# Layer 0's scan: four state groups of one channel half in a row, and B brought to SBUF by DMA instead of to PSUM by a matmul

## The chip, the cores and the metric

The kernel runs on one core of a Trainium2 chip. The metric is the device time of one launch in microseconds (us). The kernel runs four layers one after the other in a single launch; the change touches only layer 0.

## The reference

Layer 0 works on `x` of shape (4, 96, 64, 64): 4 images, 96 channels, a sequence of 4096 positions. Two Mamba blocks are applied to each image, then a 1x1 convolution, a batch norm and a residual. Only the Mamba block matters here (192 inner channels, 16 states):

```python
xs, z = jnp.split(h @ in_w, 2, axis=-1)          # h: normalised sequence
xc = silu(causal_conv(xs))                       # 4 taps
dbl = xc @ xproj_w
dt, Bm, Cm = dbl[..., :6], dbl[..., 6:22], dbl[..., 22:]
delta = softplus(dt @ dt_w + dt_b)
dA  = exp(delta[..., None] * A)                  # (b, l, 192, 16)
dBx = delta[..., None] * Bm[:, :, None, :] * xc[..., None]
hstates = scan over l of  s = dA * s + dBx
y = einsum('blds,bls->bld', hstates, Cm) + Dp * xc
return (y * silu(z)) @ out_w
```

Everything is float32. Layers 1 to 3 (another state space layer, an attention layer, a deformable convolution layer) follow and are the same in both kernels.

## The kernel before

**Units and visits.** The sequence is cut into chunks of T = 512 positions. A *unit* is one chunk of one block of one image: 4 x 2 x 8 = 64 units, in order. The 192 channels are two *halves* (`hf`) of 96; the 16 states are four *groups* (`nq`) of 4. One *visit* `v` handles one half and one group: 96 channels x 4 states = 384 rows, laid out as 3 tiles (`q`, NG = 3) of 128 partitions (32 channels x 4 states). So a unit has 8 visits, numbered `m`; the list `ORDER` says which (group, half) each is: (0,0), (0,1), (1,0), (1,1), (2,0), (3,0), (3,1), (2,1).

**What a visit does.** `xR` holds delta*xc and `dR` holds delta, each replicated four times over the partitions; both are tiles of 128 x 3 x 512 in SBUF, loaded from a DRAM buffer `spread` by six DMAs per half (`replicate`, L537). Then:

- `states_in` (L557): one TensorE matmul with a selection matrix puts the four B rows of the group on 128 partitions, `Bb`, a PSUM tile of a pool with one buffer (`pb`). Two visits in a row of the same group share it.
- `inputs` (L566, the instruction is L571): VectorE multiplies `xR` by `Bb`, broadcast over the 3 tiles: `bt`, 128 x 1536.
- `decay` (L575, L582): ScalarE computes exp(A * dR) for one tile into PSUM (`a_ps`, 3 buffers).
- `states` (L594, L598): VectorE runs the scan of one tile in place in `bt`.
- `outputs` (L602): ScalarE saves the carry (L606), GpSimd multiplies `bt` by `Cb` (L607). `Cb` is C on 128 partitions, loaded by DMA into SBUF.
- `collect` (L611): TensorE sums over the states into `yp` (L621, L624); two visits later.

`bt` has 4 buffers, so the multiplication of a visit needs the `collect` of four visits before.

**Preparation.** `prepare` (L416) computes everything a unit needs before its visits: norm, convolution (L450, 16 matmul records), the projection (L471), `dbl`, softplus, and the gate. It is a generator with some 35 steps. It puts six large products on GpSimd per unit, all 96 x 1024 tensor_tensor with both inputs in SBUF: L465, L504, L509, L517, L528, and, in `finish` (L637), L640. On VectorE it puts L440 and two L497.

**What sets the order.** The order of layer 0 is written out by hand (`manual_schedule`). The main loop (L676) walks over the visits, four slots `q` = 0..3 each: slots 0 to 2 issue a scan and the decay two ahead, slot 3 issues `collect(v - 2)`, `outputs(v)` and `inputs(v + 1)`. The steps of `prepare` are dealt out one per slot; a unit's preparation begins `AHEAD` = 14 slots before the unit ahead of it starts (`PERIOD` is 32 slots). Each engine executes its own instructions in this order; DMAs of this layer are all issued from SyncE's queue (SP), also in order.

In the slots below, (m, q) is slot q of visit m of a unit.

Of the kernel before, what the change touches and what calls it, by code (L numbers as in the profile page):

```python
# [10 lines left out]
F32 = mybir.dt.float32  # L11
# [46 lines left out]
def host_arrays(inp):  # L58
# [16 lines left out]
    for at, n, src in ((0, 6, 0), (32, 16, 6), (64, 16, 22)):  # L75
        xp[:, :, at : at + n] = inp["L0_conv_xproj_w"][:, :, src : src + n]
# [18 lines left out]
    seln = np.zeros((128, 4, 128), f)  # L95
    for n in range(4):
        seln[32 + 4 * n + p % 4, n, p] = 1
    a["c_seln"] = seln
# [241 lines left out]
def layer0(k, X):  # L340
# [6 lines left out]
    ORDER = ((0, 0), (0, 1), (1, 0), (1, 1), (2, 0), (3, 0), (3, 1), (2, 1))  # L347
    LAST = {hf: max(m for m, o in enumerate(ORDER) if o[1] == hf) for hf in range(2)}
    with ExitStack() as es:
# [11 lines left out]
        seln = k.load(wp, "c_seln", (128, NQ, 128))  # L361
# [24 lines left out]
        def pool(name, bufs, **kw):  # L386
            return scan.enter_context(tc.tile_pool(name=f"l0{name}", bufs=bufs, **kw))
# [4 lines left out]
        pm, pa = pool("pm", 2, space=PSUM), pool("pa", 3, space=PSUM)  # L392
        pb, py = pool("pb", 1, space=PSUM), pool("py", 2, space=PSUM)
# [22 lines left out]
        def prepare(b, i, ch, st, before):  # L416
# [28 lines left out]
            xc = st["xc"] = p3.tile([C, 2, T], F32, name="xc")  # L445
# [9 lines left out]
            yield  # L455
            for hf, p in enumerate(ps):
                nc.scalar.activation(xc[:, hf], p[:C], AF.Identity, bias=k.v(f"conv_b{i}{hf}"))
                yield
# [17 lines left out]
            out = dram.tile([16, T], F32, name="out_states")  # L476
            nc.sync.dma_start(out, dbl[64:80])
# [47 lines left out]
            replicate(st, 0)  # L525
# [4 lines left out]
            st["Cb"] = [cp.tile([128, T], F32, name="Cb") for _ in range(NQ)]  # L530
            for nq, t in enumerate(st["Cb"]):
                nc.sync.dma_start(
                    t, out[PS * nq : PS * nq + PS].unsqueeze(0).to_broadcast([32, PS, T])
                )
            yield

        def replicate(st, hf):  # L537

            for n, name in enumerate(("dR", "xR")):
                t = st[name, hf] = p3.tile([128, NG, T], F32, name=name)  # L540
                for q in range(NG):
                    r = 96 * hf + 32 * q
                    nc.sync.dma_start(
                        t[:, q], st["spread"][n, r : r + 32].unsqueeze(1).to_broadcast([32, PS, T])
                    )

        units = [(b, i, ch) for b in range(B) for i in range(2) for ch in range(NCH)]
        V = NT * len(units)
        sts = [{} for _ in units]
        carries, bts, Bbs, dec, skips = {}, {}, {}, {}, {}  # L550

        def at(v):

            u, m = divmod(v, NT)
            return (sts[u], units[u], *ORDER[m])

        def states_in(v):  # L557

            st, _, nq, _ = at(v)
            if v and v % NT and ORDER[v % NT - 1][0] == nq:  # L560
                Bbs[v] = Bbs[v - 1]
                return
            Bb = Bbs[v] = pb.tile([128, T], F32, name="Bb")
            nc.tensor.matmul(Bb, seln[:, nq], st["dbl"], start=True, stop=True)  # L564

        def inputs(v):  # L566

            st, _, nq, hf = at(v)
            bt = bts[v] = bp.tile([128, NG, T], F32, name="bt")
            Bb = Bbs[v]  # L570
            nc.vector.tensor_mul(  # L571
                bt, st["xR", hf], Bb.unsqueeze(1).to_broadcast([128, NG, T])
            )
# [28 lines left out]
        def outputs(v):  # L602

            st, _, nq, hf = at(v)
            bt = bts[v]
            nc.scalar.copy(carry_of(v), bt[:, :, T - 1])  # L606
            nc.gpsimd.tensor_mul(  # L607
                bt, bt, st["Cb"][nq].unsqueeze(1).to_broadcast([128, NG, T])
            )

        def collect(v):  # L611
# [11 lines left out]
            for q in range(NG):  # L623
                nc.tensor.matmul(  # L624
                    st["yp", hf][32 * q : 32 * q + 32],
                    red,
                    bt[:, q],
                    start=False,
                    stop=v % NT == LAST[hf],
                )  # L630

        def output(u, hf):

            st, (b, i, ch) = sts[u], units[u]
            nc.scalar.copy(st["xc"][:, hf], st["yp", hf])
# [24 lines left out]
        PERIOD, AHEAD = 4 * NT, 14  # L660

        with tc.manual_schedule():
# [4 lines left out]
            replicate(sts[0], 1)  # L667
            states_in(0)
# [7 lines left out]
            for v in range(V + 7):  # L676
                u, m = divmod(v, NT)
                for q in range(4):
# [4 lines left out]
                    if (m, q) in ((4, 1), (5, 0), (5, 1), (5, 3)):  # L683
                        next(task, None)
# [4 lines left out]
                    if q == 1 and v + 1 < V:  # L689
                        states_in(v + 1)  # L690
                    if q == 1 and m in (1, 2) and 0 < u <= len(units):
                        output(u - 1, m - 1)
# [10 lines left out]
                    if q == 3:  # L703
                        outputs(v)
                        if m == LAST[0] and u + 1 < len(units):
                            replicate(sts[u + 1], 1)
                        if v + 1 < V:
                            inputs(v + 1)
# [1489 lines left out]
```

## Time and profile before

| | |
|---|---|
| time, median of 3 runs | 7859.52 us (7859.1 to 7862.05) |
| profiled execution, its own time | 7854.38 us |
| its span in the trace | 7852.6 us |
| granted TensorE clock, mean | 0.815 |
| layer 0 in the span | until about 3460 us |
| visits (L571) | 512, in 64 units |

Busy time in the stretch 500 to 3300 us of the span, all of it layer 0 in its steady course (2800 us):

| engine | busy us | share |
|---|---|---|
| TensorE (matmul) | 2147.5 | 77% |
| VectorE (DVE) | 2406.6 | 86% |
| ScalarE (ACT) | 1909.9 | 68% |
| GpSimd (POOL) | 2218.7 | 79% |
| DMA engines, mean share | | 29%, 97 GB/s |

How to read it: several engines are busy most of the time and hand tiles round in a ring, so no share by itself says what a change is worth; what counts is how long a unit takes and which wait ends last in it. The product L640 comes once per unit, so its start times mark the units: from 181.27 us (the first) to 3369.7 us (the 62nd) there are 61 units, (3369.7 - 181.27) / 61 = 52.27 us each. The last two units, which have less preparation beside them, are shorter (47.5 and 35.9 us).

### The profile page before, as it was taken

What the parts mean: (1) busy time and instruction counts of PE and PEld (TensorE: products, weight loads), DVE (VectorE), ACT (ScalarE), POOL (GpSimd) and SP (SyncE); (2) the same over time, 40 slices, a digit from 0 to 9 for tenths busy, and PEclk for the clock granted to TensorE, in tenths of its full rate; (3) what the DMA queues carried; (4) which work ended last, traced back from release to release, by engine and by line L of the source; (5) the groups of instructions that cost most, each with busy time, mean ns of one, the idle gap of its engine ahead of it and who ended that gap; (6) DMA issues with size and microseconds to landing.
All of it is one profiled execution on the core that took longest, in us unless ns stands there. A gap on an engine that the chain in (4) does not pass through costs nothing.

```text
span 7852.6 us, 76871 instructions
## 1 busy us (share of the span) xinstructions
PE 5919.8 (75%) x24218; PEld 2757.7 (35%) x24218; DVE 5718.9 (73%) x8127; ACT 3944.6 (50%) x7624; POOL 4694.6 (60%) x2915
## 2 busy tenths in 40 slices
PE   5777777777777777756666989898987577777774
PEld 1222222222222222224223646455554534443432
DVE  4888888888888888865886545455454477777787
ACT  4666666666666666643332556455555212121212
POOL 3787778777887788742444434334250067777775
PEclk8888888888888888878886888888888678787886
DMA  3233223223332223234222001010100155656555
GB/s 99 101 102 103 79 101 103 98 84 101 102 103 79 101 103 103 84 115 125 80 80 67 19 11 32 1 41 2 36 8 24 40 168 158 189 152 189 158 157 172
DMA packets 424414, 720.32 MB, mean 92 GB/s; under 512 B 188150, under 2 KB 190254, under 8 KB 419763
## 3 DMA queue, kind: packets, MB, share of 16 engines
q1 hardware_dynamic: 348710, 480.74, 19.7%
q0 software_dynamic: 73968, 227.47, 10.2%
q10 hardware_dynamic: 1328, 7.20, 0.2%
q8 instruction: 193, 3.16, 0.2%
q14 instruction: 215, 1.75, 0.1%
HBM read 567.04 MB, written 97.82 MB: 85 GB/s over the span
## 4 chain that ended last, share of the span: by engine, by line
PE 30%; DVE 19%; POOL 7%; ACT 6%; issue 6%; DMA 4%; SPq 1%; DVEq 0%; POOLq 0%; ACTq 0%
POOL sm L1993 5%; PE sc_ps L1069 3%; DVE bt L598 3%; PE mm_ps L450 2%; PE pT_ps L1118 2%; DMA sm<-table,ix 2%; DVE bt L571 2%; PE o_ps L1138 2%; DVE prod L2010 2%; DVE sm L2011 1%; PE Bb L564 1%; PE mm_ps L507 1%; PE m_ps L1527 1%; PE bc_ps L319 1%; DVE lp L886 1%
## 5 line engine op out<-in xcount | busy, mean ns | idle before, releaser
L607 POOL TENSOR_TENSOR bt<-bt,Cb 128x1536 f32<-128x1536 f32 x512 | 1761.9, 3441 | 674.3 <-issue 444.9
L598 DVE TENSOR_TENSOR_SCAN bt<-a_ps,carry,bt 128x512 f32<-128x512 f32 x1536 | 1865.2, 1266 | 58.5 <-ACT a_ps L582 11.4
L1993 POOL DMA_INDIRECT sm<-table,ix x1152 | 1098.4, 953 | 742.9 <-ACT maps L1669 346.3
L582 ACT ACTIVATE a_ps<-dR,w_l_A_log 128x512 f32<-128x512 f32 x1536 | 1053.6, 687 | 345.9 <-DVE bt L598 341.6
L571 DVE TENSOR_TENSOR bt<-xR,Bb 128x1536 f32<-128x1536 f32 x512 | 889.2, 1737 | 389.6 <-issue 186.9
L564 PE MATMUL Bb<-dbl,w_c_seln 128*128 128x512 f32 x640 | 446.5, 786 | 383.4 <-DVE bt L571 383.4
L1106 POOL TENSOR_TENSOR p<-p,rs 128x392 f32<-128x392 f32 x384 | 311.6, 839 | 476.8 <-DVE rs L1104 406.1
L450 PE MATMUL mm_ps<-h,Wk 96*128 96x512 f32 x1024 | 564.5, 714 | 11.0 <-issue 6.6
L624 PE MATMUL yp<-bt,w_c_red 128*32 128x512 f32 x3072 | 559.5, 634 | 6.0 <-POOL bt L607 6.0
L471 PE MATMUL mm_ps<-xc,w_l_xp 96*128 96x512 f32 x256 | 232.8, 1064 | 290.6 <-POOL xc L465 290.6
L2031 PE MATMUL sT_ps<-ident,sd 128*128 128x128 f32 (+1 forms) x896 | 212.9, 355 | 295.8 <-DVE sd L2014 175.7
L319 PE MATMUL bc_ps<-xs,w_l_bc 96*128 96x512 f32 x384 | 241.8, 763 | 215.1 <-DVE q L913 215.1
L1093 ACT ACTIVATE p<-p,rs 128x196 f32<-128x196 f32 x768 | 342.7, 449 | 83.6 <-DVE rs L1083 83.3
L450 PEld LDWEIGHTS mm_ps<-h,Wk 96*128 96x128 f32 x1024 | 240.0, 236 | 363.2 <-issue 333.1
L564 PEld LDWEIGHTS Bb<-dbl,w_c_seln 128*128 128x128 f32 x640 | 137.2, 242 | 655.7 <-DVE bt L571 496.6
L1916 PE MATMUL yb_ps<-X,w_l_base_w 96*128 96x504 f32 (+3 forms) x576 | 311.4, 706 | 0.3 <-ACT go L1930 0.3
L2010 DVE TENSOR_TENSOR prod<-sm,cws 128x960 f32<-128x960 f32 (+1 forms) x256 | 270.8, 1058 | 55.2 <-DMA sm<-table,ix 49.5
L2032 ACT COPY sT<-sT_ps 128x512 f32<-128x512 f32 (+1 forms) x256 | 121.8, 476 | 368.1 <-PE sT_ps L2031 368.1
L1126 DVE COPY pT<-pT_ps 98x512 f32<-98x512 f32 x256 | 176.0, 687 | 155.1 <-PE pT_ps L1118 147.7
L507 PE MATMUL mm_ps<-h,w_l_z_w 96*128 96x512 f32 x256 | 226.3, 1035 | 76.3 <-ACT w L503 76.3
L890 POOL TENSOR_SCALAR q<-lp 128x1024 f32<-128x1024 f32 x48 | 133.6, 2784 | 236.4 <-DVE lp L886 236.4
L1083 DVE CUSTOM_DVE_ANT_0 p<-sc_ps,bias 128x196 f32<-128x196 f32 x768 | 233.6, 353 | 49.6 <-PE sc_ps L1069 49.3
(372 smaller groups left out, 12615.3 us busy)
## 6 DMA issues: line engine op xcount, KB each, us to landing
dR<-spread SPq DMA_DIRECT2D x384, 256.0 KB
xR<-spread SPq DMA_DIRECT2D x384, 256.0 KB
Cb<-out_states SPq DMA_DIRECT2D x256, 256.0 KB
spread<-w SPq DMA_DIRECT2D x128, 192.0 KB
spread<-dx SPq DMA_DIRECT2D x128, 192.0 KB
table<-xT SPq DMA_DIRECT2D x256, 96.0 KB
own<-vd SPq DMA_DIRECT2D x512, 36.8 KB
toep<-l_toep SPq DMA_DIRECT2D x12, 1536.0 KB
```

The costliest lines, as they stand in the source:

```text
L319: self.nc.tensor.matmul(ps[:, s], lhsT, rhs[:, s], start=k == 0, stop=k == len(terms) - 1)
L450: nc.tensor.matmul(p, Wk[:, i, t, hf], h[:, t : t + T], start=t == 0, stop=t == 3)
L564: nc.tensor.matmul(Bb, seln[:, nq], st["dbl"], start=True, stop=True)
L571: nc.vector.tensor_mul(bt, st["xR", hf], Bb.unsqueeze(1).to_broadcast([128, NG, T]))
L582: nc.scalar.activation(dec[n], st["dR", hf][:, q], AF.Exp, scale=A[:, i, nq, hf, q : q + 1])
L598: nc.vector.tensor_tensor_scan(t, dec.pop(n), t, carry_of(v)[:, q : q + 1], ALU.mult, ALU.add)
L607: nc.gpsimd.tensor_mul(bt, bt, st["Cb"][nq].unsqueeze(1).to_broadcast([128, NG, T]))
L624: nc.tensor.matmul(st["yp", hf][32 * q : 32 * q + 32], red, bt[:, q], start=False, stop=v % NT == LAST[hf],)
L1093: nc.scalar.activation(ps[n][:, h, i], ps[n][:, h, i], AF.Exp, scale=-1.0, bias=rs[n][:, 0, h, i : i + 1], accum_out=rs[n][:, 1, h, i : i ...
L1106: nc.gpsimd.tensor_tensor(ps[n][:, h], ps[n][:, h], rs[n][:, 1, h].unsqueeze(2).to_broadcast([128, 2, KW * KW]), ALU.mult,)
L1993: nc.gpsimd.indirect_dma_start(sm[u][:, t].rearrange("p q c -> p (q c)"), None, samples[m // NN % 2], bass.IndirectOffsetOnAxis(ap=ix[m][: ...
L2010: nc.vector.tensor_mul(p, v[:, :, 2:4], w_[:, :, 2:4])
```

## The change

- The visits of a unit go through the four groups of half 0 and then the four groups of half 1 (`m % NQ`, `m // NQ`); `ORDER` and `LAST` are gone.
- `states_in`, its selection matrix and its PSUM pool are gone. B rows are written to DRAM together with the C rows (one DMA of 32 rows where 16 were written before), and `broadcast` loads the 128-partition copies of both by DMA into SBUF, four `Bb` and four `Cb` per unit, 6 buffers each. `inputs` multiplies `xR` by this `Bb`.
- `dR` and `xR` have 2 buffers each instead of 3: one per half. The loads of the next unit's half 0 are issued at slot (3, 1) and those of half 1 at (7, 1).
- The matmul results of the preparation get a third PSUM buffer (`pm`).
- `AHEAD` is 24 instead of 14, so every step of the preparation comes 10 slots earlier; the steps of `finish` and `output` move to other slots.

The core of the diff (line numbers of the kernel before are those above; in the changed kernel the products and scans are L554 for L571, L581 for L598, L590 for L607, and the preparation's products L458, L497, L502, L510, L520 and L623 for L465, L504, L509, L517, L528 and L640):

```diff
-    ORDER = ((0, 0), (0, 1), (1, 0), (1, 1), (2, 0), (3, 0), (3, 1), (2, 1))
...
-        pm, pa = pool("pm", 2, space=PSUM), pool("pa", 3, space=PSUM)
-        pb, py = pool("pb", 1, space=PSUM), pool("py", 2, space=PSUM)
+        pm, pa = pool("pm", 3, space=PSUM), pool("pa", 3, space=PSUM)
+        py = pool("py", 2, space=PSUM)
...
-            out = dram.tile([16, T], F32, name="out_states")
-            nc.sync.dma_start(out, dbl[64:80])
+            rows = st["rows"] = dram.tile([2, 16, T], F32, name="rows")
+            nc.sync.dma_start(rows.rearrange("c n t -> (c n) t"), dbl[48:80])
...
-                t = st[name, hf] = p3.tile([128, NG, T], F32, name=name)
+                t = st[name, hf] = p2.tile([128, NG, T], F32, name=name)
...
+        def broadcast(st, c, nq):
+
+            name = ("Bb", "Cb")[c]
+            t = st[name, nq] = cp.tile([128, T], F32, name=name)
+            src = st["rows"][c, PS * nq : PS * nq + PS]
+            nc.sync.dma_start(t, src.unsqueeze(0).to_broadcast([32, PS, T]))
...
-            return (sts[u], units[u], *ORDER[m])
-
-        def states_in(v):
...
-            Bb = Bbs[v] = pb.tile([128, T], F32, name="Bb")
-            nc.tensor.matmul(Bb, seln[:, nq], st["dbl"], start=True, stop=True)
+            return (sts[u], units[u], m % NQ, m // NQ)
...
             bt = bts[v] = bp.tile([128, NG, T], F32, name="bt")
-            Bb = Bbs[v]
+            Bb = st["Bb", nq]
...
-        PERIOD, AHEAD = 4 * NT, 14
+        PERIOD, AHEAD = 4 * NT, 24
...
-                    if q == 1 and v + 1 < V:
-                        states_in(v + 1)
-                    if q == 1 and m in (1, 2) and 0 < u <= len(units):
-                        output(u - 1, m - 1)
+                    if q == 1 and m == 6 and u < len(units):
+                        output(u, 0)
+                    if q == 1 and m == 2 and 0 < u <= len(units):
+                        output(u - 1, 1)
+                    if u + 1 < len(units):
+                        if q == 1 and m in (3, 7):
+                            replicate(sts[u + 1], m // NQ)
+                        if q == 3 and m in (4, 5):
+                            for nq in (2 * m - 8, 2 * m - 7):
+                                broadcast(sts[u + 1], 0, nq)
+                        if q == 3 and m in (6, 7):
+                            for nq in (2 * m - 12, 2 * m - 11):
+                                broadcast(sts[u + 1], 1, nq)
```

More of the change, by code (lines that the diff above doesn't have):

```diff
@@ L74, in host_arrays @@
     xp = np.zeros((2, 192, 128), f)
-    for at, n, src in ((0, 6, 0), (32, 16, 6), (64, 16, 22)):
+    for at, n, src in ((0, 6, 0), (48, 16, 6), (64, 16, 22)):
         xp[:, :, at : at + n] = inp["L0_conv_xproj_w"][:, :, src : src + n]
@@ L94, in host_arrays @@
     a["c_red"] = red
[L95 to L98, printed above, removed]
     a["l1_toep"] = _row_pair_bands(inp["L1_conv_conv_w"])
@@ L346, in layer0 @@
     NT = 2 * NQ
-    ORDER = ((0, 0), (0, 1), (1, 0), (1, 1), (2, 0), (3, 0), (3, 1), (2, 1))
-    LAST = {hf: max(m for m, o in enumerate(ORDER) if o[1] == hf) for hf in range(2)}
     with ExitStack() as es:
@@ L360, in layer0 @@
         red = k.load(wp, "c_red", (128, 32))
-        seln = k.load(wp, "c_seln", (128, NQ, 128))
         Af = A.rearrange("p i n h q -> p (i n h q)")
@@ L443, in prepare @@
             yield
-            xc = st["xc"] = p3.tile([C, 2, T], F32, name="xc")
             ps = []
@@ L455, in prepare @@
             yield
+            xc = st["xc"] = p3.tile([C, 2, T], F32, name="xc")
             for hf, p in enumerate(ps):
@@ L524, in prepare @@
             nc.scalar.activation(gate, gate, AF.Ln, bias=k.one[:C])
-            replicate(st, 0)
             yield
@@ L529, in prepare @@
             yield
[L530 to L535, printed above, removed]
         def replicate(st, hf):
             for n, name in enumerate(("dR", "xR")):
-                t = st[name, hf] = p3.tile([128, NG, T], F32, name=name)
+                t = st[name, hf] = p2.tile([128, NG, T], F32, name=name)
                 for q in range(NG):
@@ L549, in layer0 @@
         sts = [{} for _ in units]
-        carries, bts, Bbs, dec, skips = {}, {}, {}, {}, {}
+        carries, bts, dec, skips = {}, {}, {}, {}
         def at(v):
             u, m = divmod(v, NT)
-            return (sts[u], units[u], *ORDER[m])
-        def states_in(v):
[L559 to L562, printed above, removed]
-            Bb = Bbs[v] = pb.tile([128, T], F32, name="Bb")
-            nc.tensor.matmul(Bb, seln[:, nq], st["dbl"], start=True, stop=True)
+            return (sts[u], units[u], m % NQ, m // NQ)
         def inputs(v):
@@ L607, in outputs @@
             nc.gpsimd.tensor_mul(
-                bt, bt, st["Cb"][nq].unsqueeze(1).to_broadcast([128, NG, T])
+                bt, bt, st["Cb", nq].unsqueeze(1).to_broadcast([128, NG, T])
             )
@@ L628, in collect @@
                     start=False,
-                    stop=v % NT == LAST[hf],
+                    stop=nq == NQ - 1,
                 )
@@ L666, in layer0 @@
                 pass
-            replicate(sts[0], 1)
-            states_in(0)
+            for hf in range(2):
+                replicate(sts[0], hf)
+            for c in range(2):
+                for nq in range(NQ):
+                    broadcast(sts[0], c, nq)
             inputs(0)
@@ L682, in layer0 @@
                             taken[w] += 1
-                    if (m, q) in ((4, 1), (5, 0), (5, 1), (5, 3)):
+                    if (m, q) in ((3, 1), (3, 3), (4, 1), (4, 3)):
                         next(task, None)
@@ L704, in layer0 @@
                         outputs(v)
-                        if m == LAST[0] and u + 1 < len(units):
-                            replicate(sts[u + 1], 1)
                         if v + 1 < V:
```

## The prediction

> **What bounds the kernel now.** I read the page's groups first, for the durations in layer 0. Each line gives line, engine, operation, output and inputs, count, busy us, mean ns of one, and the idle time before it.
>
> ```profile
> span 7852.6 us, 76871 instructions
> ...
> L607 POOL TENSOR_TENSOR bt<-bt,Cb 128x1536 f32<-128x1536 f32 x512 | 1761.9, 3441 | 674.3 <-issue 444.9
> L598 DVE TENSOR_TENSOR_SCAN bt<-a_ps,carry,bt 128x512 f32<-128x512 f32 x1536 | 1865.2, 1266 | 58.5 <-ACT a_ps L582 11.4
> ...
> L571 DVE TENSOR_TENSOR bt<-xR,Bb 128x1536 f32<-128x1536 f32 x512 | 889.2, 1737 | 389.6 <-issue 186.9
> L564 PE MATMUL Bb<-dbl,w_c_seln 128*128 128x512 f32 x640 | 446.5, 786 | 383.4 <-DVE bt L571 383.4
> ```
>
> Per visit VectorE has one multiplication (L571) and three scans. In the last unit, with no preparation beside it, the multiplications start at 3402.62, 3408.00, 3413.38 and 3418.76 us: an undisturbed visit takes 5.38 us. A unit adds two L497 (0.67 each), one L440 (0.74) and, in every second unit, a bn_stats (0.69): 8 x 5.38 + 1.34 + 0.74 + 0.35 = 45.5 us, against the 52.27 us that a unit takes. Next the list of waits of VectorE, from 200 to 3400 us of the span (total us, times, longest):
>
> ```profile
> DVE bt L571 <- issue: 183.8, 59, 4.4
> DVE bt L571 <- PE Bb L564: 180.7, 86, 4.0
> DVE stats L657 <- ACT X L656: 39.4, 30, 1.4
> ```
>
> The two waits ahead of L571 are 364.5 / 62 = 5.9 us per unit. In the timeline (start, duration) both kinds are one thing: Bb sits in PE's queue behind other matmuls, L644/L646 in one place and the 16 of L450 in the other, where the wait is called "issue" though Bb ended at 2049.25.
>
> ```profile
> 2028.09 1.02 PE L564 MATMUL Bb<-dbl,w_c_seln 128*128 128x512 f32 x2
> 2029.22 1.75 DVE L571 TENSOR_TENSOR bt<-xR,Bb 128x1536 f32<-128x1536 f32 x1 [3.11 <-PE Bb L564]
> ...
> 2048.12 1.13 PE L564 MATMUL Bb<-dbl,w_c_seln 128*128 128x512 f32 x2
> 2049.34 1.75 DVE L571 TENSOR_TENSOR bt<-xR,Bb 128x1536 f32<-128x1536 f32 x1 [3.41 <-issue]
> ```
>
> So layer 0 is bound by VectorE's chain plus this wait. The change removes the wait. But L571 now reads two SBUF tensors; every VectorE product of layer 0 so far reads one SBUF tensor and one from PSUM, and L571 takes 1719 to 1756 ns whatever GpSimd does. So I looked in layer 1 for VectorE products with two SBUF inputs beside GpSimd:
>
> ```profile
> 3626.89 1.20 DVE L868 TENSOR_TENSOR dl<-sp_w,dl 96x1024 f32<-96x1024 f32 x1
> 3627.06 3.65 POOL L890 TENSOR_SCALAR q<-lp 128x1024 f32<-128x1024 f32 x1 [13.84 <-DVE lp L886]
> ...
> 3666.49 2.76 POOL L890 TENSOR_SCALAR q<-lp 128x1024 f32<-128x1024 f32 x1 [6.74 <-DVE lp L886]
> 3667.41 1.22 DVE L868 TENSOR_TENSOR dl<-sp_w,dl 96x1024 f32<-96x1024 f32 x1
> ...
> 3943.91 2.76 POOL L890 TENSOR_SCALAR q<-lp 128x1024 f32<-128x1024 f32 x1 [7.04 <-DVE lp L886]
> 3944.54 1.49 DVE L868 TENSOR_TENSOR dl<-sp_w,dl 96x1024 f32<-96x1024 f32 x1
> ...
> 3634.19 2.35 POOL L872 TENSOR_TENSOR dx<-dl,xs 96x1024 f32<-96x1024 f32 x1
> 3635.22 1.87 DVE L885 TENSOR_SCALAR lp<-rl,w_l_A 128x1024 f32<-128x1024 f32 x1
> ```
>
> They exclude each other. L868 (two SBUF inputs) began 0.17 us before L890, and L890 took 3.65 us instead of 2.76: it stood until L868 was nearly done. With L890 0.63 us ahead, L868 took 1.49 instead of 1.21: held until 0.91 us into L890. With L890 0.92 us ahead neither was held. And L885 (0.75 us otherwise) took 1.87 beside GpSimd's tensor_tensor L872: held until 0.2 us before L872's end. The layer 1 products with one PSUM input (L908) show no such thing.
>
> **Part by part.** *Removed*: five Bb matmuls per unit, 5 x 2 x 0.786 = 7.9 us of PE, and with them VectorE's 5.9 us of waiting. By that alone a unit falls to 45.5 us.
>
> *Added*: the exclusion of L571 (new L554) and all of GpSimd's products. Per unit GpSimd has 8 of L607 (3.44 us) and 6 of the preparation's (2.35): 41.6 us; the multiplications are 8 x 1.73 = 13.8. Were both wholly exclusive, 55.4 us would be needed. How long a GpSimd tensor_tensor holds VectorE's read off is between two rows: by L872/L885 to 0.2 us before its end (3.2 of 3.4 us, 2.2 of 2.4), the upper end. By L868/L890, 1024 elements of one input were held 0.91 us, 0.89 ns each; with two inputs that is 2.7 us for L607 (3072 elements) and 1.8 for the others, an estimate from that row and my lower end. L885 is another kind of VectorE instruction, L890 another kind of GpSimd instruction, so neither row is nearer and I take the middle.
>
> I walk through one unit with both, in rounded durations: multiplication 1.8, scans 3.6, GpSimd's large product P 3.4, its preparation product X 2.4; P of a visit is ready 0.4 us after its scans (the carry copy). VectorE's multiplication is next in its queue at once after the scans, so it normally gets in first and P runs beside the next scans, 3.4 beside 3.6, at no cost. Cost arises where an X or a second P follows. The changed order on GpSimd is P0, three X (L497, L502, L510), P1, two X (L520, L623), P2, P3, P4, X (L458), P5, P6, P7; VectorE has the two L490 (1.3 us) after visit 0 and L433 (0.7) in visit 3. Upper end, starting with multiplication 0 at 0: scans and L490 end at 6.7, but P0 started at 5.8, so multiplication 1 waits to 9.0; 2 is ready at 14.4 and waits for the second X to 15.4; 3 is ready at 20.8, waits for P1 to 22.8; 4 is ready at 28.9, starts 29.2; 5 is ready at 34.6, waits for P3 to 37.6; 6 is ready at 43.0, waits for L458 to 45.0; 7 starts at 50.4; the next unit at 55.8. Lower end, same steps: 8.5, 14.5, 21.4, 27.5, 35.4, 42.4, 47.8, next unit 53.2. VectorE waits 10.6 or 8.0 us where it waited 5.9. With 0.35 for bn_stats: 56.15 or 53.55 us.
>
> *Moved*: ten slots earlier, the preparation sends rows, spread (x4) and the six products past other visits; the GpSimd order above includes that. On SP, rows stand at (7, 0) and may hold the half-1 loads at (7, 1) behind them; those are needed at (3, 1) of the next unit, 16 slots later. Half 0, loaded at (3, 1), is needed at (7, 3), 18 slots or over 20 us later; at the start of the kernel dR was used 3.1 us after its issue and xR 6.1. With two buffers instead of three nothing is late; without this cover up to 6 us a unit would be. The four Bb loads cost 2.55 us of SP issue (the row of four Cb) and 67 MB, 20 GB/s on top of 97; the share goes from 0.29 to 0.35. They are issued 9 or more slots ahead; cost nothing. PSUM's third buffer: nothing, since no wait on pm is in the list. At the start, multiplication 0 now waits for six half-1 loads and Bb behind the first six: 7 more of 256 KB, where six took 8.1 us (94.18 to 102.26): +9 us, once.
>
> *Sum*, over 62 full units: upper (56.15 - 52.27) x 62 + 9 = +250, lower (53.55 - 52.27) x 62 + 9 = +88 us. On the profiled execution's 7854.4 us (span 7852.6; 5 us under the median of the runs): 8104 and 7943; the middle is 8023, I say 8020.
>
> The Trainium skill, page "SBUF — State Buffer", section "Who interferes with whom", speaks against this change: a VectorE instruction with two SBUF inputs contends with a GpSimd instruction that reads SBUF, and whoever starts first holds the port for its whole instruction. L885 and the 3.65 us of L890 agree; L868 at 3667.41, not held though L890 ran 1.84 us more, does not. By the page's rule the sum would be near 8104, by the L868 row near 7943.
>
> **Rivals.** *No exclusion of this pair* (faster). For it: L868 at 3667.41 runs at full speed beside GpSimd. Against: 3.65 and 1.49. A unit falls to 45.55: (45.55 - 52.27) x 62 + 9 = -408, 7447 us. *A short hold*: GpSimd holds only half of each product (1.7 and 1.2 us). The walk gives 7.5, 12.9, 18.8, 24.9, 31.8, 38.2, 43.6, 49.0; 49.35 us, 7682. This decides from a hold of about 68%: there a unit plus the start comes out at 52.27. *GpSimd keeps the port through its queue* (much slower): a waiting multiplication gets in only when GpSimd has nothing ready. Then 2 waits through three X, P1 and two X to 26.0, and GpSimd stands later for want of scans; the next unit starts at 61.1: 8433 us. No row shows a VectorE product waiting before two queued GpSimd products.
>
> **How the numbers follow.** Forecast 0.73, own range 7943 to 8104, and up to 8170 if a third of GpSimd's present idle time behind the carry copy (197 us, 3.2 per unit) falls where neither side can work. Short hold 0.11, no exclusion 0.10, queue 0.06. The range 7680 to 8170 leaves out the last two. A measurement can tell 0.2%, 16 us. Faster: 0.10 + 0.10 of the short hold; same 0.03, from both sides of the 68%; slower 0.77.
>
> **What would show it.** In the trace after, L554 should average 2.7 to 3.1 us instead of 1.74, with a spread from 1.7 to over 4; L590 should average above 3.6 because the multiplication holds it; L581 and L565 should keep their durations; units of 53.5 to 56. L554 steady at 1.74 and units near 46 make the prediction wrong by its main step; long waits on DMA for Bb, xR or dR would show the loads mis-sized.

## The result, and the profile after

The changed kernel takes 8632.03 us (median of 4 runs, 8624.76 to 8636.61) against 7859.31 us before (median of 4, 7859.05 to 7862.05): a ratio of 1.0981, 95% interval 1.0962 to 1.1. The forecast was 8020 us, its range 7680 to 8170. The direction was right, the size was not: +773 us where +160 was forecast.

All of it lies in layer 0. The first multiplication of VectorE starts at 106.43 us (before 102.26), the last at 4221.27 (before 3441.11); behind the last the profiled executions take 4402 and 4411 us. So a unit takes 64.42 us where it took 52.27 and where 53.55 to 56.15 was forecast: (64.42 - 52.27) x 64 = 778 us.

The page's groups of the kernel after (line, engine, operation, operands, count, busy us, mean ns of one, idle time before):

```profile
span 8623.0 us, 76363 instructions
...
L590 POOL TENSOR_TENSOR bt<-bt,Cb 128x1536 f32<-128x1536 f32 x512 | 2006.1, 3923 | 827.3 <-ACT carry L589 412.8
L581 DVE TENSOR_TENSOR_SCAN bt<-a_ps,carry,bt 128x512 f32<-128x512 f32 x1536 | 1869.1, 1267 | 107.0 <-ACT a_ps L565 59.2
L554 DVE TENSOR_TENSOR bt<-xR,Bb 128x1536 f32<-128x1536 f32 x512 | 1777.7, 3472 | 21.2 <-DMA Bb<-rows 21.2
```

The scans are as long as before. The multiplication's idle time has gone (389.6 us before, 21.2 now, all at the start), but its own duration has doubled, from 1737 to 3472 ns. *The port* is short here for what a VectorE multiplication with two SBUF inputs and a GpSimd product cannot have at the same time. Time in which VectorE stands for it does not show as idle: the instruction only looks longer. That is (3.472 - 1.737) x 8 = 13.9 us per unit, in place of 5.9 us of visible waiting.

The timeline of VectorE (DVE) and GpSimd (POOL) in one unit, start and duration in us, shows how it waits:

```profile
2007.64 3.63 DVE L554 TENSOR_TENSOR bt<-xR,Bb 128x1536 f32<-128x1536 f32 x1
2009.74 3.74 POOL L502 TENSOR_TENSOR w<-w,dx 96x1024 f32<-96x1024 f32 x1
...
2013.56 2.35 POOL L510 TENSOR_TENSOR dx<-w,xc 96x1024 f32<-96x1024 f32 x1
2014.93 8.28 DVE L554 TENSOR_TENSOR bt<-xR,Bb 128x1536 f32<-128x1536 f32 x1
2015.87 3.42 POOL L590 TENSOR_TENSOR bt<-bt,Cb 128x1536 f32<-128x1536 f32 x1
2019.24 2.35 POOL L520 TENSOR_TENSOR sz<-sz,gate 96x1024 f32<-96x1024 f32 x1
2021.55 3.86 POOL L623 TENSOR_TENSOR xc<-xc,sz 96x1024 f32<-96x1024 f32 x1
```

The first multiplication gets in ahead of L502, which then stands 1.4 us. The second is ready at 2014.93, during L510; the walk of the prediction lets it in when L510 ends, at 2015.9. Instead L590 and L520, both ready behind L510, go first, each at its full speed; it ends at 2014.93 + 8.28 = 2023.21, so it gets in at 2023.21 - 1.74 = 2021.47. This repeats: from 300 to 3900 us of the span, all 49 multiplications that waited at the end of L510 were passed by L590, and all 49 again by L520; all 49 that waited at the end of the first L590 behind L458 were passed by the second. All 56 that waited at the end of L497 got in there.

One wait, costed at nothing, has also grown (list of VectorE's waits, 500 to 4000 us: total, times, longest):

```profile
DVE stats L640 <- ACT X L639: 146.7, 27, 6.5
```

Finish's bn_stats waits for X, the image, into which finish writes the unit's result. From 500 to 3300 us (43.5 units) it is 130.2 us, 3.0 per unit, against 37.9 us (0.7 per unit) before. In the same stretch the skip's tensor_scalar (L601, for the term Dp * xc) takes 6.37 us instead of 0.52, 12 times, 1.6 us per unit. Sum: 45.5 + 13.9 + 3.0 + 1.6 + 1.2 (idle time ahead of the scans) = 65.2 us, 0.8 more than the 64.4 measured.

### The profile page after: what moved, and what is told of

It reads as the page before. It is cut to its first block, busy times and chain, and to the rows that moved or that the text cites. A ratio compares the mean times of both kernels' runs of the same rounds, so it can differ in the third digit from the quotient of the medians.

```text
span 8623.0 us, 76363 instructions
## 1 busy us (share of the span) xinstructions
PE 5816.3 (67%) x23578; PEld 2625.2 (30%) x23578; DVE 6696.2 (78%) x8127; ACT 3928.5 (46%) x7624; POOL 5135.2 (60%) x2915
## 4 chain that ended last, share of the span: by engine, by line
PE 32%; DVE 30%; POOL 14%; issue 10%; ACT 8%; DMA 5%; SPq 1%; DVEq 0%; POOLq 0%; ACTq 0%
DVE bt L581 8%; DVE bt L554 7%; PE mm_ps L442 5%; POOL sm L1986 5%; PE mm_ps L629 3%; POOL xc L623 2%; PE sc_ps L1062 2%; POOL bt L590 2%; PE pT_ps L1111 2%; DMA sm<-table,ix 2%; PE yp L607 2%; PE mm_ps L464 2%; PE o_ps L1131 2%; ACT a_ps L565 2%; POOL sz L520 1%
## 5 line engine op out<-in xcount | busy, mean ns | idle before, releaser
L590 POOL TENSOR_TENSOR bt<-bt,Cb 128x1536 f32<-128x1536 f32 x512 | 2006.1, 3923 | 827.3 <-ACT carry L589 412.8
L581 DVE TENSOR_TENSOR_SCAN bt<-a_ps,carry,bt 128x512 f32<-128x512 f32 x1536 | 1869.1, 1267 | 107.0 <-ACT a_ps L565 59.2
L554 DVE TENSOR_TENSOR bt<-xR,Bb 128x1536 f32<-128x1536 f32 x512 | 1777.7, 3472 | 21.2 <-DMA Bb<-rows 21.2
L607 PE MATMUL yp<-bt,w_c_red 128*32 128x512 f32 x3072 | 681.0, 770 | 30.9 <-POOL bt L590 30.9
L500 PE MATMUL mm_ps<-h,w_l_z_w 96*128 96x512 f32 x256 | 206.4, 899 | 420.0 <-ACT w L496 420.0
L442 PE MATMUL mm_ps<-h,Wk 96*128 96x512 f32 x1024 | 479.6, 622 | 11.9 <-issue 8.2
L422 PE MATMUL mm_ps<-e,mean 96*128 96x512 f32 x128 | 132.8, 1141 | 411.2 <-ACT e L419 411.2
L629 PE MATMUL mm_ps<-xc,w_l_out_w 96*128 96x512 f32 x256 | 229.1, 1047 | 257.3 <-POOL xc L623 226.7
L458 POOL TENSOR_TENSOR xc<-xc,gate 96x1024 f32<-96x1024 f32 x64 | 160.7, 2510 | 245.9 <-issue 187.2
L442 PEld LDWEIGHTS mm_ps<-h,Wk 96*128 96x128 f32 x1024 | 198.0, 199 | 330.3 <-issue 324.8
L604 PE MATMUL yp<-xc,skip 96*96 96x512 f32 x256 | 237.7, 1032 | 65.7 <-DVE skip L601 65.7
```

The lines of the kernel that those rows point to most:

```text
L442: nc.tensor.matmul(p, Wk[:, i, t, hf], h[:, t : t + T], start=t == 0, stop=t == 3)
L554: nc.vector.tensor_mul(bt, st["xR", hf], Bb.unsqueeze(1).to_broadcast([128, NG, T]))
L581: nc.vector.tensor_tensor_scan(t, dec.pop(n), t, carry_of(v)[:, q : q + 1], ALU.mult, ALU.add)
L590: nc.gpsimd.tensor_mul(bt, bt, st["Cb", nq].unsqueeze(1).to_broadcast([128, NG, T]))
L607: nc.tensor.matmul(st["yp", hf][32 * q : 32 * q + 32], red, bt[:, q], start=False, stop=nq == NQ - 1,)
L629: nc.tensor.matmul(p, out_w[:, i, hf], st["xc"][:, hf], start=False, stop=hf == 1)
```

## Experiments

The theories named in the expectations: P, the port (the multiplication with two SBUF inputs and GpSimd's products exclude each other); D, the added loads; O, the new order and the places of finish. K, Q and S came later and are explained there. The runs of parts 1 to 4 stand beside a kernel before of 7864 us, those of the later parts beside one that itself took 8443 to 8463 us (granted clock 0.788 to 0.794, against 0.813 to 0.816). So each ratio is against the kernel before that ran beside it, and kernels of different parts are compared by layer 0's unit, taken as (last multiplication - first) / 511 x 8. That comparison holds because the longer time lies behind layer 0: from the last multiplication to the end it is 4972 to 5028 us in every profile of the later parts, 4399 to 4418 in the earlier ones. For layer 0 an estimate from part 11: its first two versions took 37 and 52 us more than the kernel before beside them, 0.6 and 0.8 us per unit, and have units of 52.9 and 53.3; that leaves 52.4 and 52.5 for the kernel before there, where 52.27 was profiled. What makes the later layers longer there is not shown.

**1. B back in PSUM, the order kept.**

```diff
+            Bb = Bbs[v] = pb.tile([128, T], F32, name="Bb")
+            nc.tensor.matmul(Bb, seln[:, nq], st["dbl"], start=True, stop=True)
-            Bb = st["Bb", nq]
+            Bb = Bbs.pop(v)
```

(eight matmuls per unit, no loads of B, two PSUM buffers for the preparation as before, and finish's places as in the next run.)

> The changed kernel's order, but B again by a matmul into PSUM (one PSUM buffer, eight matmuls per unit, two PSUM buffers for the preparation); the last two steps of finish come at (5, 1) and (5, 3). Theory P (two SBUF inputs make the multiplication wait for GpSimd): its mean falls from 3.47 us to 1.74 us, the 14 us of waiting per unit go, a wait behind Bb on TensorE comes back (5.9 us per unit in the kernel before); units of 47 to 53 us, 7550 to 7900 us. Theory O (the order of the visits and the preparation ten slots earlier cost the time): multiplication 1.74 us, but units stay above 60 us, over 8350 us.

Measured: 8119.66 us, ratio 1.0325 (1.0307 to 1.0343), unit 56.4.

```profile
L565 DVE TENSOR_TENSOR bt<-xR,Bb 128x1536 f32<-128x1536 f32 x512 | 891.1, 1740 | 566.2 <-PE Bb L558 453.5
```

The multiplication is at 1740 ns again, as P said, and the unit far from O's 60 us. But 56.4 is above P's 47 to 53: B on TensorE is now waited for longer (566.2 us of idle time ahead of the multiplication, 389.6 in the kernel before).

**2. Finish's last two steps later.**

```diff
-                    if (m, q) in ((3, 1), (3, 3), (4, 1), (4, 3)):
+                    if (m, q) in ((3, 1), (3, 3), (5, 1), (5, 3)):
```

> The changed kernel, only with the last two steps of finish at (5, 1) and (5, 3) instead of (4, 1) and (4, 3), and the four steps of pooled at visit 6 instead of 7. Theory F (in every second unit bn_stats holds VectorE behind the convolution on TensorE, 147 us in 27 units): that wait goes, and up to 2.7 us per unit with it, 8460 to 8520 us. Its rival: the time was hidden in what the multiplication waits for anyway, 8600 us or more.

Measured: 8594.2 us, 1.0931 (1.0913 to 1.0949), unit 63.8 (the four steps of the pooling also come a visit earlier). The wait for X from 500 to 4000 us falls from 146.7 to 94.7 us, the multiplication stays at 3460 ns. A small part: the time falls by 38 us, where theory F had 112 to 172.

**3. B by DMA, but multiplied out of PSUM.** The run before, and ScalarE copies the loaded B into a PSUM buffer (which the preparation gives up, two instead of three):

```diff
+            Bbs[v] = pb.tile([128, T], F32, name="Bp")
+            nc.scalar.copy(Bbs[v], st["Bb", nq])
```

> As the kernel with finish later, B by DMA into SBUF as in the changed kernel, then copied by ScalarE into one PSUM buffer (0.58 us, eight per unit), which the multiplication reads. Theory P: multiplication 1.74 us, no Bb on TensorE, units of 46 to 49 us, 7480 to 7680 us. Theory D (the 67 MB of B by DMA into SBUF slow the work): no better than the changed kernel's 8632 us by more than the finish's 170 us.

Measured: 7960.91 us, 1.0129 (1.0108 to 1.015), unit 54.0. With the same order and more traffic, one operand's move to PSUM takes 633 us off run 2, so D falls and P holds. But 54.0 is neither 45.5 nor in P's 46 to 49. The page's multiplication, and the longest entry of VectorE's waits (500 to 4000 us):

```profile
L560 DVE TENSOR_TENSOR bt<-xR,Bp 128x1536 f32<-128x1536 f32 x512 | 887.9, 1734 | 55.1 <-ACT Bp L553 29.5
```

```profile
DVE bt L587 <- ACT a_ps L571: 173.8, 123, 3.7
```

ScalarE has eight copies of 582 ns more per unit, and VectorE now waits for its a_ps.

**4. A shorter product on GpSimd.** One of the three tiles of each large product is multiplied, two thirds of that product are left out:

```diff
+            nc.gpsimd.tensor_mul(bt[:, 0], bt[:, 0], st["Cb", nq])
```

> The changed kernel, but GpSimd multiplies by C only the first of the three tiles of a visit (leaves two thirds of that product out): 1.2 us instead of 3.44, GpSimd's work per unit 24 us instead of 42. Theory P: the multiplication's mean falls from 3.47 us to below 2.4 us and units to 50 to 55 us, 7750 to 8050 us. Theory D or O: mean and time stay within 3% of the changed kernel's.

Measured: 7924.72 us in one run, unit 53.4, as P expected:

```profile
L590 POOL TENSOR_TENSOR bt<-bt,Cb 128x512 f32<-128x512 f32 x512 | 948.2, 1854 | 1072.5 <-ACT carry L589 713.5
...
L554 DVE TENSOR_TENSOR bt<-xR,Bb 128x1536 f32<-128x1536 f32 x512 | 1191.5, 2327 | 21.3 <-DMA Bb<-rows 21.3
```

The multiplication itself is unchanged, and takes 1.15 us less (3472 to 2327 ns) because GpSimd does less.

**5. Two SBUF inputs in the old order.** The kernel before, with a copy by ScalarE (`sz` has two buffers instead of three):

```diff
+            Bs = Bbs[v] = p2.tile([128, T], F32, name="Bs")
+            nc.scalar.copy(Bs, Bb)
```

> The kernel before in its own order, with one thing taken from the change: ScalarE copies the broadcast B from PSUM to SBUF, and VectorE's multiplication reads the copy, so that both of its inputs lie in SBUF. No loads of B by DMA, and the visits alternate between the halves as before. Theory P (the multiplication now waits for GpSimd's products, and some of them pass it): its mean rises from 1.74 us to 2.8 to 3.5 us, the unit from 52.3 to 57 to 61 us, the time to 8150 to 8400 us. Theory O (the order and the places of finish make the loss): the multiplication stays at 1.74 us and the time within 60 us of 7860, but for the copies on ScalarE.

Measured: ratio 1.1311 (1.1284 to 1.1338), unit 69.8, the multiplication at 2632 ns from 500 to 3300 us: 7.2 us per unit of port. So the port's cost does not need the new order. The multiplication is below the 2.8 to 3.5 us that P expected and the unit above its 57 to 61, and the size is not clean: ScalarE's copy stood 698.8 us of these 2800 waiting for B on TensorE, and VectorE 312.8 us for the copy.

**6. The same product in three pieces.**

```diff
+            for q in range(NG):
+                nc.gpsimd.tensor_mul(bt[:, q], bt[:, q], st["Cb", nq])
```

> The kernel after with GpSimd's product of each visit issued as three products of 128x512, the same work in all. If the multiplication waits for the product in progress and up to two whole ones behind it (theory 3), the pieces shorten its wait from 14 us per unit to 5 to 8: 7950 to 8300 us with the multiplication's mean at 2.2 to 2.7 us, although GpSimd issues three times as many. If GpSimd keeps the port until its queue is empty, however the queue is cut (theory 2), the mean stays above 3.3 us and the time above 8550 us. If the order alone cost it (theory O), no change: 8630 us.

Measured: ratio 1.091 (1.0887 to 1.0933), unit 64.38, the same as after; the multiplication at 3214 ns from 500 to 3300 us, just under theory 2's 3.3 us and far above theory 3's 2.2 to 2.7. Being passed is not counted in products: cutting them in three takes 2.1 us per unit off the port's wait (13.9 to 11.8) and nothing off the unit.

**7. The port by itself.** Two probes without the computation; the second asks what the first left open. A *boundary* is the moment at which one GpSimd product ends and the next begins: *open* if the waiting multiplication gets in there, *closed* if it is passed.

> A probe that leaves the whole computation out (it copies x to the output). Each row releases GpSimd and VectorE together: GpSimd then runs a short queue (one to five of the kernel's products with both inputs in SBUF, 128x1536 or 96x1024, or the clipping tensor_scalar on 128x1024, with nothing between them), VectorE a delay of 16 to 2560 elements on PSUM and then the kernel's multiplication of 128x1536, with two SBUF inputs or, as a control, one in PSUM. Each row is run five times. Theory 1 (my walk: the multiplication gets in at the end of the product in progress): it never lasts over 1.74 + 3.44 us, whatever is queued. Theory 2 (GpSimd keeps the port as long as its queue is ready): with five products it lasts until the last one ends, 10 to 17 us. Theory 3 (the product in progress and up to two more, as the trace of the kernel after looks): 1.74 + at most 9 us, the same with four products as with five. The control with PSUM lasts 1.74 us in all three. For the clipping, the first two allow up to 2.76 us of wait; the trace of layer 1 before, where a VectorE operation got in 0.92 us into it, says less.

> A second probe that leaves the whole computation out, for the rule by which VectorE's multiplication (two SBUF inputs) gets in between GpSimd's products. The first probe: it got in behind 128x1536 when 128x1536 or 96x1024 followed, and behind 96x1024 when 96x1024 followed, but not where 128x1536 followed 96x1024. Theory K (GpSimd's parts work ahead: partitions 96 to 127, which a 96-row product leaves idle, begin the next 128-row product at once and hold the port meanwhile): a 96x1536 product behind 96x1024 lets it in, a 128x1024 one ahead of 128x1536 lets it in, 128x1536 behind 96x1536 doesn't, and behind 96x1024 and then several 128x1536 it gets in only at the end of the last one, since those partitions stay ahead. Theory S (it is the size of the next product, or the time that it takes to issue, not its rows): 128x1024 ahead of 128x1536 keeps it out and 96x1536 behind 96x1024 does too. In neither does a wait end before the end of the product in progress.

Measured, as the time from the start at which the multiplication is ready and gets in (its end less 1.74 us); S is 96x1024 and ends at 2.48 when first, L is 128x1536 and ends at 3.55:

| GpSimd's queue | ready at | gets in |
|---|---|---|
| L | 0.37, 0.88, 1.42, 1.95, 2.49, 3.02 | 3.43 each time |
| S | 0.37, 0.88, 1.42, 1.95 | 2.35 each time |
| L L L L L | 0.88 and 2.48 | 3.43 |
| S S S S S | 0.88 | 2.35 |
| S L S S | 0.88 and 1.95 | 5.72 |
| S L L L; S L L L L | 0.89 | 12.47; 15.85 |
| S S L S | 3.28 | 4.65 |
| S S S L S S | 0.88 | 4.65 |
| 128x1024, L | 0.89 | 2.35 |
| S, 96x1536, S | 0.89 | 2.35 |
| 96x1536, L, S | 0.89 | 3.48 |
| S, 128x1024, S, 128x1024, S | 0.89 | 2.40 |
| S, a copy of 96x3, L | 0.89 | 5.85 |
| clipping, 128x1024, from 0.26 to 3.03 | 0.37 | 1.17 |
| L L L L L, one input in PSUM | 0.89 | 0.89 |

Two rows of the second probe's timeline, S L L L L and 128x1024 L:

```profile
333.71 2.34 POOL L75 TENSOR_TENSOR small<-small,G 96x1024 f32<-96x1024 f32 x1
...
334.46 16.70 DVE L83 TENSOR_TENSOR M<-R,Bs 128x1536 f32<-128x1536 f32 x1
336.01 13.54 POOL L71 TENSOR_TENSOR big<-big,Cb 128x1536 f32<-128x1536 f32 x4
```

```profile
44.46 2.34 POOL L77 TENSOR_TENSOR wide<-wide,G 128x1024 f32<-128x1024 f32 x1
...
45.21 3.20 DVE L83 TENSOR_TENSOR M<-R,Bs 128x1536 f32<-128x1536 f32 x1
46.75 4.93 POOL L71 TENSOR_TENSOR big<-big,Cb 128x1536 f32<-128x1536 f32 x1
```

One small product of 96 rows at the head makes the multiplication wait through four large ones; with 128 rows at the head it gets in at that product's end (2.35), and the large product stands instead (4.93). Theories 1, 2 and 3 all fall: equal rows behind each other let it in at the first boundary, and behind a 96x1024 product it waits as long as 128x1536 ones follow. Theory S falls on 128x1024. K fits every row: by it rows 96 to 127, which have nothing to do in a 96-row product, are ahead with the next 128-row one and hold the port across the boundary. Behind S they stay 2.3 us ahead through all the L that follow. In S S L they are done with L (3.4 us) before the second S ends (4.77), so that boundary is open. In S S S L even the boundary between the first two S is closed, by an L two places further on. Where the product behind S is 128x1024, no longer than S, they are done with it when S ends, and the boundary is open (2.40): 96 rows alone do not close it. One expectation drawn from K failed. It was 96x1536 ahead of L: I wrote that it would keep VectorE out, but the upper rows need just as long for L as the others for 96x1536, so both end together (3.48), as K should have told me.

**8. GpSimd's six large preparation products on 128 rows.** The decisive run in the kernel: the 96-row tiles get 32 rows of zeros, and GpSimd's products run over all of them.

```diff
-            nc.gpsimd.tensor_mul(xc, xc, gate)
+            nc.gpsimd.tensor_mul(xcF, xcF, gateF)
```

(and so for the five others; xcF is the tile of 128 rows, xc its first 96.)

> The kernel after with one thing changed on GpSimd: its six 96x1024 operations per unit run on all 128 partitions (rows 96 to 127 are zeros, written once; the results are the same). The operations keep their length, their order and their places. Theory K (rows 96 to 127, left idle by a 96-row operation, let GpSimd's upper partitions begin the next 128-row product early, so that the port is never free between the two): all partitions then end together, the multiplication gets in at the end of the product in progress, as my walk assumed, and the unit falls from 64.4 us to 54.5 to 57.5 us, the multiplication's mean from 3.47 to 2.5 to 3.0 us. Theory Q (GpSimd keeps the port as long as its next operation is ready, whatever its rows): the unit stays at 63.5 to 65 us.

Measured: ratio 1.083 (1.0802 to 1.0858). The groups of VectorE from 500 to 3300 us:

```profile
L595 DVE TENSOR_TENSOR_SCAN bt<-a_ps,carry,bt 128x512 f32<-128x512 f32 x1058 | 1294.7, 1269 | 300.8 <-ACT a_ps L579 268.7 <-DVE bt L568 0.5
L568 DVE TENSOR_TENSOR bt<-xR,Bb 128x1536 f32<-128x1536 f32 x353 | 864.8, 2450 | 22.7 <-DMA dR<-spread 20.3 <-PE yp L621 2.4
```

The multiplication falls from 3476 ns in this stretch to 2450, its wait from 13.9 to 5.7 us per unit. The place shown above now looks so:

```profile
2032.37 2.34 POOL L524 TENSOR_TENSOR dx<-w,xc 128x1024 f32<-128x1024 f32 x1
2033.74 2.59 DVE L568 TENSOR_TENSOR bt<-xR,Bb 128x1536 f32<-128x1536 f32 x1
2034.67 4.95 POOL L604 TENSOR_TENSOR bt<-bt,Cb 128x1536 f32<-128x1536 f32 x1
```

2.59 us instead of 8.28: it gets in at the end of the product in progress, ahead of the large one. From 300 to 3900 us no product passes a waiting multiplication any more; 50 of 50 get in here. So being passed is shown to come from the 96-row products. But the unit is 63.2 us, not 54.5 to 57.5: scans now wait 6.1 us per unit for a_ps (268.7 us) and bn_stats 4.4 for X (195.3 us). Most of the 8.2 us that the port gave back were spent in another queue: 45.5 + 5.7 + 6.1 + 4.4 is 61.7 of the 63.2. TensorE's granted clock in this stretch was 0.69 (0.72 in the kernel after, 0.84 in the kernel before); what a lower clock adds to these waits was not separated.

**9. Why the second row is kept out in the kernel.**

> A third probe that leaves the whole computation out. GpSimd runs 96x1024, 128x1536, 96x1024, 96x1024 (or with a second 128x1536 in third place, or 128x1024 in place of each 96x1024); the first 128x1536 also waits for a small copy on ScalarE, which comes 0.5 to 2.6 us after the start, as the carry does in the kernel. VectorE's multiplication arrives in the first product. Theory K: with the copy early the upper partitions are ahead and the first boundary keeps VectorE out; the later the copy, the less they are ahead, and where it comes just before the end of the 96x1024 they end just behind the others and the boundary behind the 128x1536 keeps VectorE out too, as in the kernel. With the copy later than the end of the first product VectorE gets in there. With 128 rows throughout it gets in at the first boundary whatever the copy. If the copy's time makes no difference, K does not explain that boundary.

Measured: with S L S S and the copy done 0.57 to 2.05 us after the start the multiplication got in at 5.72, behind L, in 27 of 28 tries (in the other, the first, the copy came only at 4.94, and it got in on arrival at 3.66); with S L L S at 9.10. With the copy at 2.27 or 2.48 it got in at 2.35, behind S. With 128 rows, at 2.35 whatever the copy. So the boundary is open where the large product is ready 0.2 us or less ahead of the small one's end (2.48), and closed from 0.4 us. That agrees with K; its other expectation, that a copy shortly before the end would close the boundary behind L too, did not come.

**10. The places of finish on top of the 128 rows.** Run 8 with run 2's slots; then run 8, and the kernel after, with the slots that the kernel before has for the four steps (the pooling a visit earlier in all three).

```diff
-                    if (m, q) in ((3, 1), (3, 3), (4, 1), (4, 3)):
+                    if (m, q) in ((4, 1), (5, 0), (5, 1), (5, 3)):
```

> The kernel after with GpSimd's operations on 128 rows and finish's last two steps two visits later (slots (5,1) and (5,3), the pooling a visit earlier). If the two causes, port and finish, are all that was missing from my walk: the unit falls from 63.2 to 55 to 58 us, the multiplication's mean stays at 2.4 to 2.6 us. If the order of the visits costs something else (TensorE or ScalarE late by themselves): 60 to 63 us.

> The kernel after with GpSimd's operations on 128 rows and all four steps of finish in the slots that the kernel before gives them ((4,1), (5,0), (5,1), (5,3)). If the places of finish are what is left beside the port, ScalarE's wait at finish's copy of X goes (9.3 us to under 3), VectorE's wait for a_ps falls from 7.2 to under 3 us per unit, and the unit from 62.2 to 54.5 to 58 us, which is what my sum had for the port alone. If the order of the visits is what makes a_ps late: 60 us or more.

> The kernel after with only the four steps of finish put where the kernel before has them; GpSimd's operations keep their 96 rows. The port's waits stay (the multiplication's mean 3.3 to 3.5 us), so the unit stays at 62.5 to 64.5 us. Under 60 us would say that the places of finish were the larger cause and the port the smaller.

Measured: ratios 1.0721 (1.0667 to 1.0776), 1.0706 (1.0672 to 1.0741) and 1.1028 (1.1003 to 1.1053); units 62.2, 62.3 and 66.2. The first two expectations, 55 to 58 and 54.5 to 58 us, failed, and the numbers fall in the rivals' ranges; the third, 62.5 to 64.5, failed upwards, with the multiplication at 3919 ns. From 500 to 3300 us, in run 8 with run 2's slots, the waits that end in VectorE's:

```profile
ACT X L645 <- PE mm_ps L643: 419.6, 45, 9.3
...
DVE bt L595 <- ACT a_ps L579: 322.8, 111, 4.8
```

and with the slots of before:

```profile
ACT xc L463 <- PE mm_ps L643: 485.7, 45, 11.5
...
DVE bt L595 <- ACT a_ps L579: 173.1, 45, 7.1
```

In both, ScalarE stands some 9 to 11 us in every unit, at whatever it has next that needs TensorE, and a_ps is queued behind. With run 2's slots TensorE stands at finish's matmul L643, which waits for GpSimd's product L637 (262.3 us, 39 times), the end of the bunch L510 to L637. With the old slots L643 waits for no one itself: TensorE stands ahead of it, at the convolution L454, which waits for a small GpSimd operation on `h` (L439, 194.2 us, 39 times; L437, 28.1) that is queued behind the same bunch:

```profile
PE mm_ps L454 <- POOL h L439: 194.2, 39, 5.2
```

So moving finish moves the wait from one line to another; with the old slots the port's wait is also larger again (the multiplication at 3075 ns).

**11. The good part alone.** Three versions of the kernel before, with its order: B by DMA into three SBUF buffers and copied by ScalarE into PSUM (`sz` has two buffers instead of three); the selection matmul in slot 0; the matmul directly behind the multiplication that frees its buffer.

```diff
-            nc.tensor.matmul(Bb, seln[:, nq], st["dbl"], start=True, stop=True)
+            nc.scalar.copy(Bb, Bss[v])
```

```diff
-                    if q == 1 and v + 1 < V:
+                    if q == 0 and v + 1 < V:
                         states_in(v + 1)
```

```diff
                             inputs(v + 1)
+                        if v + 2 < V:
+                            states_in(v + 2)
```

> A version that tries to keep the good part alone: the kernel before with its order of visits, B broadcast by DMA into three SBUF buffers (one load per change of group, three visits ahead), and ScalarE copying each into the one PSUM buffer that the multiplication reads. TensorE's selection matmuls are gone, the multiplication still has one input in PSUM. If the 5.9 us per unit that VectorE waited for TensorE's B are won and ScalarE's five copies per unit (about 0.6 us each) cost VectorE nothing: 7500 us. If the copies delay a_ps and the wait only changes its name: 7750 to 7900. Theory D (the loads of B by themselves slow the kernel): above 7900 us. The multiplication's mean stays at 1.74 us in all of these.

> The kernel before with one edit: the selection matmul of the next visit's B is written at the start of a visit (slot 0, ahead of the preparation's matmuls of slots 0 and 1) and not in slot 1. Nothing of the change is in it; it asks whether the 5.9 us per unit that VectorE waited for B on TensorE, the wait that the change was to remove, are the matmul's place in TensorE's queue. If they are: 2 to 4 us per unit less, a ratio of 0.97 to 0.985 to the kernel before. If TensorE is late as a whole (its queue is behind whatever the order): 0.995 to 1.005.

> As the run before it, but the matmul is written directly behind the multiplication that frees its one PSUM buffer, at the end of the visit before (slot 3), the earliest place that one buffer allows. If the place is what counts, B is never late: 4 to 5.9 us per unit less, a ratio of 0.95 to 0.97. If TensorE then stands waiting for VectorE's multiplication with the preparation's matmuls queued behind it, the gain is smaller or gone: 0.99 to 1.02.

Measured: ratios 1.0053 (1.0031 to 1.0075), 1.0061 (1.0039 to 1.0084), 1.009 (1.0067 to 1.0112); units 52.9, 53.3, 53.3. None beats the kernel before. In the first no wait for B on TensorE is left, but the multiplication has 138.8 us (500 to 3300) behind ScalarE's xc, which waits for the convolution on TensorE: the wait only changed its name. In the second, VectorE's idle time ahead of the multiplication is 203.5 us in that stretch (315.1 in the kernel before), but its scans wait 99.7 us (38.9) and L497 66.3 us (none): an earlier B shifts TensorE's lateness to the preparation's results; the third has much the same (208.8, 99.4 and 65.1 us). So the gains that the last two expected, 2 to 5.9 us per unit, did not come. How much of these waits is a lower clock is not separated (0.83 in this stretch in the last two, 0.77 in the first, 0.84 in the kernel before).

## Why the prediction was wrong, step by step

- *VectorE's chain, 45.5 us per unit*: held for the durations (scan 1267 ns, a_ps 686, an undisturbed multiplication 1.74 us). As a time that a unit would reach with the wait for B removed it did not: without the port's wait runs 1 and 3 have 56.4 and 54.0 us, because TensorE and ScalarE are late next. Both have work that the chain has not (eight matmuls, eight copies), so no run shows 45.5, and the price of the rival *no exclusion*, 7447 us, which rests on it, is not borne out.
- *The 5.9 us of waiting for B go*: they did (21.2 us of idle time are left, all at the start). *L554 excludes GpSimd's products*: it does (runs 3, 4, 7).
- *How long one product holds the port*: the upper end. The multiplication got in 0.13 us before the product's end at all six arrival times, so 2.7 and 1.8 us, from a row of clipping, were wrong; clipping does hold only its first 0.9 of 2.76 us. That also ends the rival *short hold*. The rule of the Trainium skill, page "SBUF — State Buffer", section "Who interferes with whom", that the first holds the port for its whole instruction, agrees with the tensor_tensor rows and not with the clipping (in at 1.17, held to 3.03 by the rule).
- **The step that failed**: in the walk, "multiplication 1 waits to 9.0", "3 ... waits for P1 to 22.8" and the others let it in at the end of the product in progress. With 96-row products ahead of 128x1536 ones it is passed. That term of the sum was 8.0 to 10.6 us per unit and measured 13.9, and 1.6 more at the skip's tensor_scalar, which the walk left out (that this too is the port is argued: in run 8 it takes 1.35 us). With 128 rows, where the walk's rule holds, the term measured 5.7.
- **The second step that failed**: the sum lets a unit end with VectorE's chain and the port, and puts VectorE's waits for what TensorE and ScalarE make at nothing. In run 8, with the walk's rule made true, the unit is still 63.2 us, because the scans wait 6.1 us for a_ps and bn_stats 4.4 for X. So the passing is what filled the time in the kernel after, but without it the forecast of 53.55 to 56.15 us would not have held either. Added up, the port with the skip was 4.9 to 7.5 us short, X 3.0 and the scans 1.2: 9.1 to 11.7, for a unit that was missed by 8.3 to 10.9.
- *The rival "GpSimd keeps the port through its queue"*, given 0.06 and 8433 us, had the nearest time and the right kind of event: in the kernel up to two further products. The nearness of its time is luck in part, since its rule is too general: five equal products let the multiplication in after the first. I had set it low because no row of before showed a VectorE product waiting before two queued ones; in layer 0 no row could, since no VectorE product there reads two SBUF tensors.
- *Finish's moved steps, costed at nothing*: 3.0 us per unit of waiting for X, against 0.7. Run 2 won 0.7 us of it back.
- *Loads, buffers and PSUM at nothing*: right as far as VectorE's waits tell; the only one for DMA ahead of the multiplication is 21.2 us at the start. The start itself cost 4.2 us, 9 were forecast.
- *The marks*: L590 above 3.6 us held (3.92), scans and a_ps held; L554 at 2.7 to 3.1 us (3.47) and units of 53.5 to 56 (64.4) failed.

What stays open: why L520 also passed, 49 of 49 times, where the probes let VectorE in behind the large product; and what a unit would take if TensorE's wait for the end of GpSimd's bunch were gone. The waits name that bunch as the origin; no run removed or moved it.

## What to carry to other kernels

Before an operand moves from PSUM to SBUF, see what the other engine at that port has queued, not only what it is running: equal operations in a row let the waiting one in between them (in at 2.35 us behind 96x1024, at 3.43 behind 128x1536), a 96-row one with a longer 128-row one behind it does not (5.72). A stall for the port shows as a longer instruction, so compare the means of the same line before taking shorter idle time for a gain. And when a wait is cured, expect the unit to fall only to the next late queue: here taking 8.2 us per unit of port away brought 1.2.

## What the runs showed of the hardware

- GpSimd does not keep its partitions in step from one instruction to the next, as far as the boundaries tell: a 96x1024 product with a ready 128x1536 one behind it closed the boundary (S L, in at 5.72), even from two places further back (S S S L, in at 4.65 instead of 2.35); with 128x1024 behind it the boundary was open (2.40), and with 128 rows throughout none was closed. That rows 96 to 127 run ahead is inferred from these times; no record shows rows apart.
- A multiplication with two SBUF inputs could be held 15 us (S L L L L: ready at 0.89, in at 15.85), with one input in PSUM not at all beside five L or five S (in on arrival at 0.89), nor in the kernel beside the mixed ones (run 1, mean 1740 ns).
- Widening six operations from 96 to 128 rows cost GpSimd nothing by itself: 96x1024 takes 2.34 us in the probe, 128x1024 also 2.34.
